# Layer 3 experts: the second product of each pass by seven block products in place of eight

## The chip, the cores and the metric

The kernel runs on one core of a Trainium2 chip. A core has five engines that work side by side: TensorE (matmuls; the trace shows its weight loads as a lane of their own), VectorE, ScalarE, GpSimd and SyncE (here it only issues transfers). The data lie in on-chip memory (SBUF), the results of matmuls in accumulation banks (PSUM), and everything large in the chip's main memory, from where DMA brings it. The metric is the device time of one execution in microseconds. The time of the kernel before is the median of three runs, 3683.46 us (3682.76 to 3685.95).

## The reference, cut to what matters

The whole computation has four layers on 4096 tokens of 256 channels. The change is in the last one, the mixture of experts of layer 3:

```python
TOP_K = 2                                  # x: 4096 tokens x 256, E = 8 experts, hidden size 1024
top_w, top_i = top_k(xf @ Wg + bg, TOP_K); top_w = softmax(top_w)
w_dense = sum(one_hot(top_i, E) * top_w[..., None], axis=1)
for e in range(E):
    h = gelu(xf @ W1[e] + b1[e], approximate=False)
    out = out + w_dense[:, e:e+1] * (h @ W2[e] + b2[e])
```

Each token goes to two of eight experts. An expert is two matrix products: 256 to 1024 with a gelu behind it (the first product), then 1024 to 256 (the second product), a bias, and the token's weight. The kernel computes in float32.

## The kernel before, in words

The kernel sorts the tokens by expert ahead of the experts' work (`route`, `tile_table`): 8192 pairs of token and expert stand in a table `xs` in main memory, each expert's rows together. `experts` then goes over passes of 256 rows each (`MT = 256`, so `NI = 2` blocks of 128 tokens). There is room for 39 passes; the first 36 (`MOST`) always run, the others only where the counts of tokens ask for them, and here they don't.

One pass, in `expert_tiles`, has these parts:

- `load(i)` issues three transfers on SyncE, in the order of that queue: 256 rows `x`, the expert's `w1` (1028 KB in the page) and `w2` (1152 KB), two passes ahead. `w1` and `w2` have three buffers each, so a load waits until the pass that read the buffer last is done with it.
- `turn(x)` (L1928, L1930): four 128x128 transposes on TensorE, one copy on VectorE to `f_xT`.
- `first(xT, w1)` (L146 with `f_h_ps`, L1940): eight chunks of 128 hidden units. A chunk is two matmul calls of 256 columns into half a bank of `f_h_ps`, then one activation on ScalarE (gelu and bias) to `f_h`. Two chunks share one bank, there are three banks, and a matmul into a bank waits for the activation that reads the other half of it.
- `where(i, x)` (L1948 to L1956): nine tiny VectorE operations which work out each row's weight `f_wgt` and its destination `f_at`.
- `second` (L146 with `f_y_ps`, L1964, L1966, L1967): for each of two blocks of 128 tokens eight accumulating matmul calls, with 128 hidden units by 128 tokens of `f_h` as the loaded weights and 256 columns of `f_w2` streamed past them; one VectorE addition of the bias over 128x512; two ScalarE scalings by the rows' weights; and two indirect transfers from GpSimd's queue, which scatter the rows into `ys`.

The loop at the end of `expert_tiles` is skewed by one pass: in the round of pass i TensorE does the first product of pass i, the transposes of pass i+1 and the second product of pass i-1. The build puts the instructions of each engine into an order by its own plan, so that order differs in places from the source: it is the order in which each engine, strictly one after the other, executes. `where` for example stands one round early, and L1948 waits for rows `x` whose load is issued in the same round.

After the last pass the rows of `ys` are read back, added to the tokens, transposed and written out.

A float32 matmul call shows in the trace as two records (two weight loads, two matmuls): the 16 calls of a second product are "x32". A record's duration runs to the modelled end of the pipeline, so the pace is read from the starts of successive records, not from the durations.

Of the kernel before, what the change touches and what calls it, by code (L numbers as in the profile page):

```python
# [10 lines left out]
F32 = mybir.dt.float32  # L11
# [3 lines left out]
ALU = mybir.AluOpType  # L15
# [4 lines left out]
P = 128  # L20
C = 256
# [28 lines left out]
NI = MT // P  # L50
# [30 lines left out]
def bc(ap, axis, n):  # L81

    ap = ap.unsqueeze(axis)
    shape = list(ap.shape)
    shape[axis] = n
    return ap.to_broadcast(shape)


class Net:
# [1813 lines left out]
    def expert_tiles(self, S, tiles, wp, ps):  # L1903
        nc, A = self.nc, self.A
        L, tab = S["L"], S["tab"]
        hidden = 256 if L == 2 else 1024
        KH = hidden // P
        ahead = 3 if L == 2 else 2
        why = "worked out from counts of tokens"

        def load(i):
            e = nc.values_load(tab[0:1, 0, i : i + 1], engines=[mybir.EngineType.SP], min_val=0, max_val=(NE - 1) * P,
                               skip_runtime_bounds_check_because=why)
            row = nc.values_load(tab[0:1, 1, i : i + 1], engines=[mybir.EngineType.SP], min_val=0, max_val=NE * N - MT,
                                 skip_runtime_bounds_check_because=why)
            x = wp.tile([P, NI, CX], F32, tag="x", name="f_x", bufs=ahead + 3)
            nc.sync.dma_start(out=x, in_=self.xs[bass.ds(row, MT), :].rearrange("(i p) c -> p i c", p=P))  # L1917
            w1 = wp.tile([P, 2 * hidden + KH], F32, tag="w1", name="f_w1")
            nc.sync.dma_start(out=w1, in_=A[f"f{L}_w1"][bass.ds(e, P), :])
            w2 = wp.tile([P, KH * C + C], F32, tag="w2", name="f_w2")  # L1920
            nc.sync.dma_start(out=w2, in_=A[f"f{L}_w2"][bass.ds(e, P), :])
            return x, w1, w2

        def turn(x):
            p = ps.tile([P, 2, MT], F32, tag="x", name="f_x_ps", bufs=2)
            for k in range(2):
                for i in range(NI):
                    nc.tensor.transpose(p[:, k, i * P : (i + 1) * P], x[:, i, k * P : (k + 1) * P], self.ident)  # L1928
            xT = wp.tile([P, 2, MT], F32, tag="xT", name="f_xT")
            nc.vector.tensor_copy(xT, p)  # L1930
            return xT

        def first(xT, w1):
            h = wp.tile([P, KH, MT], F32, tag="h", name="f_h")
            for m in range(KH):
                if m % 2 == 0:
                    p = ps.tile([P, 2, MT], F32, tag="h", name="f_h_ps", bufs=3)
                q = p[:, m % 2, :]
                self.mm(q, [(w1[:, kt * hidden + m * P : kt * hidden + (m + 1) * P], xT[:, kt, :]) for kt in range(2)])
                nc.scalar.activation(h[:, m, :], q, AF.Gelu, bias=w1[:, 2 * hidden + m : 2 * hidden + m + 1])  # L1940
            return h

        def where(i, x):

            tl = lambda tag, dt=F32: wp.tile([P, NI], dt, tag=tag, name="f_" + tag, bufs=4)
            first, second, to, wgt, at = tl("first"), tl("second"), tl("to"), tl("wgt"), tl("at", I32)
            op = nc.vector
            op.tensor_scalar(first, x[:, :, C + 3], S["ex"][:, i : i + 1], None, ALU.is_equal)  # L1948
            op.tensor_scalar(second, first, -1.0, 1.0, ALU.mult, ALU.add)
            op.tensor_tensor(wgt, second, x[:, :, C + 2], ALU.mult)  # L1950
            op.tensor_scalar(second, second, float(N), None, ALU.mult)
            op.tensor_tensor(to, x[:, :, C], second, ALU.add)
            op.tensor_tensor(to, to, S["in"][:, i, :], ALU.mult)
            op.tensor_tensor(at, to, S["off"][:, i, :], ALU.add)
            op.tensor_tensor(first, first, x[:, :, C + 1], ALU.mult)
            op.tensor_tensor(wgt, wgt, first, ALU.add)  # L1956
            return at, wgt

        def second(i, h, w2, at, wgt):
            p = ps.tile([P, NI, C], F32, tag="y", name="f_y_ps", bufs=2)  # L1960
            y = wp.tile([P, NI, C], F32, tag="y", name="f_y")
            for k in range(NI):
                self.mm(p[:, k, :], [(h[:, m, k * P : (k + 1) * P], w2[:, m * C : (m + 1) * C]) for m in range(KH)])
            nc.vector.tensor_tensor(y, p, bc(w2[:, KH * C :], 1, NI), ALU.add)  # L1964
            for k in range(NI):
                nc.scalar.mul(y[:, k, :], y[:, k, :], wgt[:, k : k + 1])  # L1966
                nc.gpsimd.indirect_dma_start(  # L1967
                    out=self.ys_parts[(i % 4) * NI + k], in_=y[:, k, :], in_offset=None,
                    out_offset=bass.IndirectOffsetOnAxis(ap=at[:, k : k + 1], axis=0),
                )  # L1970

        tiles = list(tiles)
        ld = {i: load(i) for i in tiles[:ahead]}
        xT = turn(ld[tiles[0]][0])
        to = where(tiles[0], ld[tiles[0]][0])
        done = None
        for i in tiles:
            if i + ahead <= tiles[-1]:
                ld[i + ahead] = load(i + ahead)
            x, w1, w2 = ld.pop(i)  # L1980
            h = first(xT, w1)
            now = (i, h, w2) + to
            if i < tiles[-1]:
                xT = turn(ld[i + 1][0])
                to = where(i + 1, ld[i + 1][0])
            if done is not None:
                second(*done)
            done = now
        second(*done)
# [518 lines left out]
```

## Time and profile before

| what | value |
|---|---|
| time, median of three | 3683.46 us |
| span of the profiled run | 3747.9 us |
| experts of layer 3, first matmul to last matmul | 3172.7 to 3696 us of that span |
| one round in the steady part (start of `f_h_ps` to the next start) | 14.49 us |
| of it: first product, transposes, second product | 7.14, 0.44, 6.91 us |
| matmul records of 128x256 in each product of the stage | 1152 |
| VectorE busy in a round | 17% |
| ScalarE busy in a round | 30% |
| GpSimd busy in a round | 14% |
| DMA engines busy in a round | 52% |

The profiled run is longer than the timed ones; the shares and durations of a stage are what is read from it. A row of the timeline gives the start in us, the length in us, the engine, line and operation, output and inputs, the tile's shape, the number of merged instructions, and in brackets how long the engine had been idle and what ended that. A row of the groups gives the busy time, the mean duration in ns, and the idle time ahead of the group with its releasers. A row of the windows gives, for a stretch of the span, the busy time of each engine with the number of instructions, the granted clock of TensorE, the share of the DMA engines and GB/s.

### The profile page before, as it was taken

The numbers are of one execution on the slowest core, as the hardware profiler recorded it, in microseconds if no ns is written. First come the engines' busy times: TensorE is split into PE (matmuls) and PEld (weight loads), VectorE is DVE, ScalarE is ACT, GpSimd is POOL, SyncE is SP. The second block draws the span as 40 slices with busy tenths as digits, with TensorE's granted clock in tenths as the row PEclk, the third lists the DMA queues.
The fourth block names the chain that finished last, engine by engine and source line by source line (L and its number), as shares of the span: only waits on it lengthen the run. The fifth ranks groups of instructions, "written<-read, shape, count | busy, mean of one in ns | idle before, by whom it ended". The sixth has DMA issues, their size and how long they took to land. (4 is left out here: it accounts for less than half of the span.)

```text
span 3747.9 us, 60403 instructions
## 1 busy us (share of the span) xinstructions
PE 3391.5 (90%) x22708; PEld 2386.9 (64%) x22708; DVE 2183.0 (58%) x5386; ACT 1389.2 (37%) x2845; POOL 1412.2 (38%) x1403
## 2 busy tenths in 40 slices
PE   6989999999997788887786967999999996999997
PEld 4433333333343688855665755888888885888886
DVE  6756656666565477778544557777777775111111
ACT  5544343343432566433332333222222222323231
POOL 1038888888885355534223433000000001111110
PEclk9999999999998899999886989999999997999998
DMA  1014414401013322200013865233223322545454
GB/s 57 3 28 115 132 38 119 124 24 41 21 41 101 108 68 74 77 19 1 13 38 127 262 213 208 86 101 96 93 88 101 97 90 110 196 179 204 180 202 166
DMA packets 160979, 378.33 MB, mean 101 GB/s; under 512 B 17377, under 2 KB 75490, under 8 KB 151458
## 3 DMA queue, kind: packets, MB, share of 16 engines
q1 hardware_dynamic: 136450, 318.96, 26.5%
q0 software_dynamic: 13056, 35.93, 2.5%
q10 hardware_dynamic: 11168, 19.42, 1.5%
q8 instruction: 185, 3.03, 0.3%
q14 instruction: 120, 0.98, 0.1%
HBM read 273.96 MB, written 100.29 MB: 100 GB/s over the span
## 5 line engine op out<-in xcount | busy, mean ns | idle before, releaser
L584 POOL TENSOR_TENSOR l_sm<-l_sc,mask 128x512 f32<-128x512 f32 (+3 forms) x624 | 770.0, 1268 | 120.0 <-ACT l_sc L574 117.6
L578 DVE TENSOR_TENSOR l_sm<-l_s,mask 128x256 f32<-128x256 f32 (+3 forms) x1248 | 492.5, 448 | 301.5 <-PE l_s L568 291.8
L574 ACT COPY l_sc<-l_s 128x384 f32<-128x384 f32 (+3 forms) x896 | 367.7, 461 | 558.5 <-PE l_s L568 543.6
L568 PE MATMUL l_s<-l_q,l_k 32*128 32x384 f32 (+2 forms) x3584 | 424.9, 514 | 7.4 <-ACT l_sc L574 4.1
L1826 POOL DMA_INDIRECT xs<-f_n,f_to x64 | 63.3, 990 | 789.0 <-DVE a_qt L2138 577.5
L146 PE MATMUL f_h_ps<-f_xT,f_w 128*128 128x256 f32 x1440 | 345.4, 388 | 15.6 <-DVE f_xT L1930 7.7
L1967 POOL DMA_INDIRECT ys<-f_y,f_at x144 | 138.7, 963 | 576.6 <-ACT f_y L1966 531.4
L146 PE MATMUL f_y_ps<-f_w,f_h 128*128 128x256 f32 x1440 | 328.5, 379 | 0.0
L568 PEld LDWEIGHTS l_s<-l_q,l_k 32*128 32x128 f32 x3584 | 165.6, 183 | 241.4 <-issue 124.1
L146 PEld LDWEIGHTS f_h_ps<-f_xT,f_w 128*128 128x128 f32 x1440 | 266.0, 192 | 83.7 <-ACT f_h L1940 21.0
L146 PEld LDWEIGHTS f_y_ps<-f_w,f_h 128*128 128x128 f32 x1440 | 268.6, 190 | 33.8
L2186 ACT ACTIVATE a_e<-a_e 128x512 f32<-128x512 f32 x256 | 156.8, 629 | 242.2 <-DVE a_e L2159 234.9
L953 DVE TENSOR_TENSOR l_pr<-l_vk,l_w_ps 128x1280 f32<-128x1280 f32 x128 | 186.5, 1481 | 55.8 <-PE l_acc_ps L957 37.7
L1940 ACT ACTIVATE f_h<-f_h_ps,f_w 128x256 f32<-128x256 f32 x360 | 163.7, 468 | 133.8 <-PE f_h_ps L146 132.1
L957 PE MATMUL l_acc_ps<-ident,l_pr 128*128 128x128 f32 x1600 | 198.0, 278 | 9.3 <-POOL l_pr L948 9.2
L957 PEld LDWEIGHTS l_acc_ps<-ident,l_pr 128*128 128x128 f32 x1600 | 184.5, 144 | 15.7 <-POOL l_pr L948 11.0
L1966 ACT ACTIVATE f_y<-f_y,f_wgt 128x256 f32<-128x256 f32 x144 | 65.3, 500 | 330.1 <-DVE f_y L1964 298.8
L611 PE MATMUL l_a_ps<-l_sm,l_v 128*32 128x512 f32 (+3 forms) x1408 | 178.7, 530 | 1.6 <-POOL l_sm L584 1.5
L2170 PE MATMUL a_sa_ps<-a_q,a_kt 128*128 128x256 f32 x512 | 155.4, 385 | 18.6 <-DMA a_kt<-a_kd 9.6
L611 PE MATMUL l_b_ps<-l_sm,l_v 128*32 128x256 f32 (+2 forms) x2176 | 171.5, 376 | 0.5 <-POOL l_sm L584 0.5
L2174 ACT COPY a_u<-a_sa_ps 128x256 f32<-128x256 f32 x128 | 47.6, 372 | 328.2 <-PE a_sa_ps L2170 325.0
L1964 DVE TENSOR_TENSOR f_y<-f_y_ps,f_w 128x512 f32<-128x512 f32 x72 | 49.8, 691 | 193.4 <-PE f_y_ps L146 187.5
(498 smaller groups left out, 6266.7 us busy)
## 6 DMA issues: line engine op xcount, KB each, us to landing
a_kt<-a_kd SPq DMA_DIRECT2D x128, 512.0 KB
f_w<-in_f_w SPq DMA_DIRECT2D x36, 1152.0 KB
f_w<-in_f_w SPq DMA_DIRECT2D x36, 1028.0 KB
xs<-zero SPq DMA_DIRECT2D x8, 4160.0 KB
l_vk<-vt SPq DMA_DIRECT2D x180, 128.0 KB
f_x<-xs SPq DMA_DIRECT2D x72, 260.0 KB
f_w<-in_f_w SPq DMA_DIRECT2D x36, 384.0 KB
l_rcp<-l_recd SPq DMA_DIRECT2D x48, 256.0 KB
```

Source lines behind the costliest of these rows:

```text
L146: self.nc.tensor.matmul(out, lhsT, rhs, start=(i == 0), stop=(i == len(pairs) - 1))
L568: nc.tensor.matmul(s[pair, j], k[hp, key * P : (key + 1) * P], qs[hp], start=True, stop=True)
L574: nc.scalar.copy(sc[:, j], s[1, j])
L578: nc.vector.tensor_tensor(sms[0][:, j, at : at + t * wide].rearrange("p (t n) -> p t n", n=wide), part[:, which, :], mask, ALU.mult)
L584: nc.gpsimd.tensor_tensor(sms[1][:, :, at : at + t * wide].rearrange("p j (t n) -> p j t n", n=wide), part[:, :, which, :], bc(mask, 1, 2) ...
L611: nc.tensor.matmul(out, v[:, key, hp], sms[pair][:, j, base + lo * wide : base + hi * wide], start=not seen[nm], stop=(left[nm] == 0 and h ...
L953: nc.vector.tensor_tensor(pr, vk, bc(held["w"][:, j, dy], 3, D), ALU.mult)
L957: nc.tensor.matmul(acc[:, m, j, :], pf[:, dx, m * P : (m + 1) * P], self.ident, is_transpose=True, start=(j == 0 and dy == 0 and dx == 0 a ...
L1940: nc.scalar.activation(h[:, m, :], q, AF.Gelu, bias=w1[:, 2 * hidden + m : 2 * hidden + m + 1])
L1967: nc.gpsimd.indirect_dma_start(out=self.ys_parts[(i % 4) * NI + k], in_=y[:, k, :], in_offset=None, out_offset=bass.IndirectOffsetOnAxis(a ...
L2170: mm = lambda out, i, right: nc.tensor.matmul(out, A[i], right, start=True, stop=True)
L2186: nc.scalar.activation(e[:, i : i + 3 : 2], e[:, i : i + 3 : 2], AF.Exp, scale=1.0 / 16.0)
```

## The change

The second product is a 256x1024 by 1024x256 product. Cut in two along the tokens, the hidden units and the output channels it is 2x2 blocks times 2x2 blocks: eight block products as usual, or seven by Winograd's form of Strassen's scheme, with sums of blocks ahead of and behind the products. The "blocks" of hidden units are the first four and the last four chunks of 128.

- `sides(w2)`: four sums of weight blocks (`f_wt`, 128x512 each) on GpSimd, once for each pass.
- `seven`: four sums of blocks of hidden units (`f_hs`, 128x512 each) on VectorE; seven block products of four matmul calls each, 128 columns wide, into two banks `f_ya_ps` and `f_yb_ps`; then a copy on ScalarE and five additions on VectorE which join the products to `f_y`.
- The bias is a VectorE addition of its own on `f_y` (128x512, both operands in SBUF). The scalings and the scatter stay.
- Layer 2's experts keep the second product as it was.

```diff
+        def sides(w2):
+            if L == 2:
+                return None
+            wt = wp.tile([P, 4, KH // 2, P], F32, tag="wt", name="f_wt", bufs=2)
+            b = w2[:, : KH * C].rearrange("p (i m j n) -> p i m j n", i=2, j=2, n=P)
+            for out, x, y in ((0, b[:, 0, :, 1], b[:, 0, :, 0]), (1, b[:, 1, :, 1], wt[:, 0]), (2, b[:, 1, :, 1], b[:, 0, :, 1]),
+                              (3, b[:, 1, :, 0], wt[:, 1])):
+                nc.gpsimd.tensor_tensor(wt[:, out], x, y, ALU.subtract)
+            return wt
+
+        def seven(h, w2, wt, y):
+            hs = wp.tile([P, 4, KH // 2, P], F32, tag="hs", name="f_hs", bufs=2)
+            a = h.rearrange("p (i m) (j n) -> p i m j n", i=2, n=P)
+            nc.vector.tensor_tensor(hs[:, 0], a[:, 0, :, 1], a[:, 1, :, 1], ALU.add)
+            nc.vector.tensor_tensor(hs[:, 1], hs[:, 0], a[:, 0, :, 0], ALU.subtract)
+            nc.vector.tensor_tensor(hs[:, 2], a[:, 0, :, 0], a[:, 0, :, 1], ALU.subtract)
+            nc.vector.tensor_tensor(hs[:, 3], a[:, 1, :, 0], hs[:, 1], ALU.subtract)
...
+            pa = ps.tile([P, 4, P], F32, tag="ya", name="f_ya_ps", bufs=2)
+            pb = ps.tile([P, 4, P], F32, tag="yb", name="f_yb_ps")
+            for out, x, z in (
+                (pa[:, 0], a[:, 0, :, 0], b[:, 0, :, 0]), (pb[:, 2], a[:, 1, :, 0], b[:, 1, :, 0]), (pb[:, 1], a[:, 1, :, 1], wt[:, 3]),
+                (pa[:, 2], hs[:, 0], wt[:, 0]), (pa[:, 1], hs[:, 1], wt[:, 1]), (pa[:, 3], hs[:, 2], wt[:, 2]), (pb[:, 0], hs[:, 3], b[:, 1, :, 1]),
+            ):
+                self.mm(out, [(x[:, m], z[:, m]) for m in range(KH // 2)])
...
+            flat = y.rearrange("p k (j n) -> p (k j) n", n=P)
+            nc.scalar.copy(u1, pa[:, 0])
+            nc.vector.tensor_tensor(flat[:, 0], u1, pb[:, 2], ALU.add)
+            nc.vector.tensor_tensor(u2, u1, pa[:, 1], ALU.add)
+            nc.vector.tensor_tensor(u, pa[:, 2:4], bc(u2, 1, 2), ALU.add)
+            nc.vector.tensor_tensor(flat[:, 3], u[:, 1], pa[:, 2], ALU.add)
+            nc.vector.tensor_tensor(flat[:, 1:3], u, pb[:, 0:2], ALU.add)
 
-        def second(i, h, w2, at, wgt):
-            p = ps.tile([P, NI, C], F32, tag="y", name="f_y_ps", bufs=2)
+        def second(i, h, w2, wt, at, wgt):
             y = wp.tile([P, NI, C], F32, tag="y", name="f_y")
-            for k in range(NI):
-                self.mm(p[:, k, :], [(h[:, m, k * P : (k + 1) * P], w2[:, m * C : (m + 1) * C]) for m in range(KH)])
-            nc.vector.tensor_tensor(y, p, bc(w2[:, KH * C :], 1, NI), ALU.add)
+            if L == 3:
+                seven(h, w2, wt, y)
+                nc.vector.tensor_tensor(y, y, bc(w2[:, KH * C :], 1, NI), ALU.add)
+            else:
+                p = ps.tile([P, NI, C], F32, tag="y", name="f_y_ps", bufs=2)
+                for k in range(NI):
+                    self.mm(p[:, k, :], [(h[:, m, k * P : (k + 1) * P], w2[:, m * C : (m + 1) * C]) for m in range(KH)])
+                nc.vector.tensor_tensor(y, p, bc(w2[:, KH * C :], 1, NI), ALU.add)
...
-            now = (i, h, w2) + to
+            now = (i, h, w2, sides(w2)) + to
```

In the order that the build gives each engine, the sums of weights for a pass stand on GpSimd in the round of its own first product, ahead of the scatters of the pass whose second product has just ended. The sums of hidden units stand on VectorE at the end of the same round's first product. So both are placed one round ahead of the products that read them.

## The prediction

> **What bounds the kernel now.** First the page's engine totals and its 40 slices of 93.7 us, to see who is full in the stage that the change touches (slices 34 to 39).
>
> ```profile
> PE 3391.5 (90%) x22708; PEld 2386.9 (64%) x22708; DVE 2183.0 (58%) x5386; ACT 1389.2 (37%) x2845; POOL 1412.2 (38%) x1403
> ...
> PE   6989999999997788887786967999999996999997
> PEld 4433333333343688855665755888888885888886
> DVE  6756656666565477778544557777777775111111
> ```
>
> TensorE is at 9 from slice 34 on, VectorE at 1. A window of the steady part says it without rounding (columns: PE, weight loads, VectorE, ScalarE, GpSimd, clock, DMA share, GB/s):
>
> ```profile
> 3300.00:3400.00 100.00, 100.00 (x471) 85.28 (x470) 16.94 (x77) 30.24 (x69) 13.54 (x14) 1.00 0.53 194
> ```
>
> A hundred per cent busy isn't yet peak pace, so next the timeline of one round:
>
> ```profile
> 3414.22 7.31 PE L146 MATMUL f_h_ps<-f_xT,f_w 128*128 128x256 f32 x32
> 3414.42 0.69 DVE L1964 TENSOR_TENSOR f_y<-f_y_ps,f_w 128x512 f32<-128x512 f32 x1 [4.06 <-PE f_y_ps L146]
> 3415.19 0.91 ACT L1966 ACTIVATE f_y<-f_y,f_wgt 128x256 f32<-128x256 f32 x2 [7.65 <-DVE f_y L1964]
> 3415.97 0.97 POOL L1967 DMA_INDIRECT ys<-f_y,f_at  x1 [12.26 <-ACT f_y L1966]
> 3416.01 0.81 ACT L1940 ACTIVATE f_h<-f_h_ps,f_w 128x256 f32<-128x256 f32 x2
> 3416.51 4.61 PEld L146 LDWEIGHTS f_h_ps<-f_xT,f_w 128*128 128x128 f32 x22 [0.38 <-ACT f_h L1940]
> 3421.36 0.60 PE L1928 MATMUL f_x_ps<-ident,f_x 128*128 128x128 f32 x4
> 3421.80 7.07 PE L146 MATMUL f_y_ps<-f_w,f_h 128*128 128x256 f32 x32
> ...
> 3423.77 0.16 DVE L1954 TENSOR_TENSOR f_at<-f_to,f_off 128x2 int32<-128x2 f32 x1 [0.75 <-DMA ys<-f_y,f_at]
> 3428.71 7.31 PE L146 MATMUL f_h_ps<-f_xT,f_w 128*128 128x256 f32 x32
> ```
>
> From starts: first product 3421.36-3414.22 = 7.14 us, transposes 0.44, second product 3428.71-3421.80 = 6.91, round 14.49. 6.91/32 is 0.216 us a record; the first product has as many records, so 7.14-6.91 = 0.23 us of it is standstill: the 0.38 at the weight loads, for the first activation, which stands on ScalarE behind the two scalings L1966. Nothing else holds the round: TensorE's pace sets it.
>
> What the new products will cost is read elsewhere, where float32 matmuls already stream 128 columns past fresh 128x128 weights:
>
> ```profile
> 1661.31 1.95 PE L146 MATMUL a_u_ps<-wg_bd,a_vT 128*128 128x128 f32 x16
> 1663.09 7.91 PE L146 MATMUL a_qkv_ps<-w_qkv,a_nT 128*128 128x512 f32 x24
> ```
>
> (1663.09-1661.31)/16 = 0.111 us a record, weight loads included.
>
> **What the skill says.** The Trainium skill, "TensorE: Matmul & The Clock Gate", section "Back-to-back issue gap", gives N/2.4 + 2.5 ns between matmuls. The trace agrees if a float32 record takes two cycles a column: 512/2.4+2.5 = 215.8 (216 here), 256/2.4+2.5 = 109.2 (111 here). The same section warns that with weight loads in the stream a bf16 matmul of 128 columns comes every 81 ns, not 56; section "LDWEIGHTS (loading the stationary operand)" gives columns/1.2, so 107 ns for 128. At 111 ns a float32 load just fits behind its predecessor: no room, but no loss in the trace. "SBUF — State Buffer", section "Who interferes with whom", says that a VectorE operation with two SBUF inputs contends with a GpSimd operation that reads SBUF, and one with a single SBUF input doesn't. The trace agrees; it shows such a pair, where VectorE's 128x256 takes 0.69 in place of 0.42 (L2190's mean is 424 ns):
>
> ```profile
> 2239.32 0.45 POOL L2150 TENSOR_TENSOR a_vs<-a_vs 128x128 f32<-128x128 f32 x1
> 2239.36 0.69 DVE L2105 TENSOR_TENSOR a_ks<-a_ks 128x256 f32<-128x256 f32 x1
> ```
>
> **The change part by part.** I set t = 0 at the first matmul of a round's first product; the round's second product ends at about 13.6.
>
> *TensorE.* Out: 32 records of 0.216 = 6.91 us. In: 7 products x 4 calls x 2 records = 56 of 0.1117 (mean of 0.111 and the 112 ns that most gaps in that row measure) = 6.25. Saved 0.66 us a pass, 36 passes: 23.8 us. It is an eighth of the columns less the fixed cost of 24 more records. All of it is on the path. Bounds: 0.109 a record (the transposes' pace, 0.44/4) would save 0.80; the warning above, taken as 81/56 x 0.109 = 0.158, would cost 1.9. I take 0.1117, since it is measured for this type and shape.
>
> *Sums of hidden units.* Four VectorE operations of 128x512, 0.69 each (L1964's row) = 2.8 us a round, and nobody waits: in the built order they stand a round ahead of their products, two just before the copy `f_xT` (L1930), two behind it. L1930 moves from about 8.5 us into the round to about 9, and TensorE wants `f_xT` at 13.6. Cost nothing, hidden by the second product.
>
> *Sums of weights.* Four GpSimd operations of 128x512. Nearest row: L1431, 1046 ns (L584, beside VectorE, 1160). So 4.2 to 4.6 us, with the contention up to 5.3. They begin when the buffer of two passes ago is free, at t = -0.7, and end at 3.6 to 4.6. Their reader comes a round later: no cost by themselves. But the two scatters stand behind them on GpSimd and move from t = 1.75 and 3.0 to about 4.4 and 5.7. Who waits for those? L1954, for its buffer, about 6.2 us behind the second scatter's start (3417.25 to 3423.77, less its own issue: here at t = 9.4), now at about 11.9. Behind L1954 on VectorE are the additions that join the products, due at 13.3. It holds by 1.4 us.
>
> *Joining the products.* Before: 0.69 us (L1964), scalings from t = 0.97. After: the copy on ScalarE waits for all four regions of `f_ya_ps`, finished 8 records before the end: t = -0.7. Then copy 0.27 (a 128x128 copy, L574's smallest form, 269 ns), 0.29 (128x128 on VectorE, L578's form, 286), 0.42 (128x256, L2159), 0.29, 0.29, 0.42, with some overlap of neighbours (about 0.08 each, seen in back-to-back rows): t = 1.2. Those have one SBUF input. The bias addition has two, beside GpSimd's sums: 0.69 alone, plus a wait of 0 to one GpSimd operation (1.05); I take 0.5. It ends at t = 2.4 (1.9 to 3.0), the scalings 0.1+0.91 later at 3.4 (2.9 to 4.0).
>
> *What queues behind that on ScalarE.* In the built order two activations now stand ahead of the scalings, and the third (second half of the first bank) behind. The two ahead remove the 0.23 us standstill. The third ends at 3.4+0.45 = 3.8 (3.3 to 4.4); TensorE needs it for the sixth chunk at 5 x 0.864 = 4.3, its weight load 0.2 sooner. So no wait in the middle, 0.3 at the upper end. I take a first product of 7.0 us.
>
> *Loads.* `w2`'s buffer is free after the bias addition: the three loads issue 1.4 us later, from t = 2.3. They are wanted a round later or more; `x` lands about 8.5 in place of 7, and L1948 with the nine tiny operations still ends before 12. The bytes stay, so DMA goes from 52% to about 55%.
>
> *Sum.* Round: 7.0+0.44+6.25 = 13.69 against 14.49. Over 36 second products 23.8; over 35 first products (0.23-0.09) x 35 = 4.9 more; the last pass ends with a longer joining chain, about 1 us lost. 23.8+4.9-1 = 27.7, say 27: **3656 us**.
>
> **Rivals.**
>
> *A: the joining chain stops TensorE.* Contention on more than the bias addition puts the scalings 0.5 us later; then the sixth chunk stands 0.3 to 0.5 us. Two engines stand between the products and the activations where it was one; against it, five of the six operations have a PSUM input. First product 7.3 to 7.4: 23.8-0.2x35-1 = 16, time 3667.
>
> *B: slower than before, by GpSimd.* If a weight sum takes 1.6 us (1.16 with the slowdown of 0.69/0.42), four take 6.4, the second scatter starts at 7.5, L1954 comes at 13.7, the joining moves by 0.5 and all behind it, and standstill reaches 1 us a round: 23.8-0.8x35-1 = -5, time 3689. For it: a queue of three engines in a ring. Against: VectorE has at most one two-SBUF operation while the sums run.
>
> *C: slower, by weight loads.* There are 56 loads in place of 32, and a load fills its record. At 0.14 us a record the second product takes 7.84: +0.93x36-4 = +29, time 3713. Against: the 111 ns measured.
>
> **How the numbers follow.** The forecast has 0.64 (no standstill to 0.2), A 0.22, B 0.09, C 0.05. The fast end is no standstill and 0.109 a record: (0.80+0.2)x36-1 = 35, but with 0.1117 it is 31, 3652; I put the low end at 3650. The upper end takes in A with a margin: 3673. B and C are left out. Faster by over 0.2% (below 3676): 0.86, with all of A bar a tail; within: 0.05; slower: 0.09, from B and C less their mild forms.
>
> **What would show it.** The second product: 56 records with starts 0.111 to 0.113 apart, 6.25 us from its first to the next first product. The first product 6.9 to 7.1 us; more, with weight loads idle for an activation, is A. On VectorE the bias addition at 0.7 to 1.5 us, the joins near 0.29 and 0.42. On GpSimd sums of 1.05 to 1.25; above 1.5, and L1954 idle for the scatter until the second product's end, is B. Records spaced at 0.13 or more are C. It would be wrong if something I hold for hidden, the copy `f_xT`, a weight sum or a load, turned up as the last release of TensorE.

## The result, and the profile after

The changed kernel takes 3663.2 us (median of four runs, 3658.9 to 3665.8), the kernel before 3684.6 in the same comparison: ratio 0.9941, 95% interval 0.9924 to 0.9958. It is 21 us faster; 3656 was forecast, 3650 to 3673 as the range.

First the page of the changed kernel, engine totals and slices, as shown of before:

```profile
PE 3325.9 (91%) x23572; PEld 2364.7 (65%) x23572; DVE 2371.5 (65%) x5710; ACT 1399.9 (38%) x2881; POOL 1615.8 (44%) x1547
...
PE   6989999999999688978696968999999996999997
PEld 4443334333333488865585746888888885988986
DVE  6756656656566467779675566777777776655552
...
POOL 1028889888897255545334442000000001555552
```

VectorE and GpSimd are at 5 in the stage where they stood at 1. GpSimd's slices before:

```profile
POOL 1038888888885355534223433000000001111110
```

TensorE still shows a 9, so the window of the steady part is needed (same columns as before):

```profile
3300.00:3400.00 100.00, 98.53 (x658) 89.34 (x658) 53.30 (x141) 34.54 (x80) 54.27 (x44) 1.00 0.55 201
```

TensorE now has 1.5 us of gaps in 100, which it had not before. From the starts of the products, 33 steady rounds can be laid side by side:

| us | before | after |
|---|---|---|
| second product, every round | 6.91 | 6.25 |
| first product | 7.15 (first three 7.10) | 6.93 in 21 rounds, 7.67 to 7.69 in 11, 7.2 in one |
| round | 14.49 | 13.62 in 21, 14.37 in 11, 13.89 in one |
| the 33 rounds together | 478.1 | 457.9 |
| first matmul of the stage to its last second-product matmul | 523.2 | 501.6 |

The stage explains the result (-21.6 us: -20.3 in the rounds (20.2 between the rounded sums), -1.4 at the end, +0.1 at the start). But the rounds are of two kinds. Here is a short one, from the end of its predecessor to its second product (start, length, engine, operation, idle time before and releaser). The line numbers have moved: L1967 is now the sums of weights, L1974 to L1977 are the sums of hidden units, L1991 to L1996 the copy and the additions that join the products (the joins), L2002 the bias, L2009 the scalings, L2010 the scatters.

```profile
3167.96 0.16 DVE L1954 TENSOR_TENSOR f_at<-f_to,f_off 128x2 int32<-128x2 f32 x1 [1.01 <-DMA ys<-f_y,f_at]
...
3168.41 2.49 POOL L1967 TENSOR_TENSOR f_wt<-f_w 128x512 f32<-128x512 f32 x2 [5.42 <-PE f_ya_ps L146]
3168.41 0.27 ACT L1991 COPY f_u<-f_ya_ps 128x128 f32<-128x128 f32 x1 [5.38 <-PE f_ya_ps L146]
...
3169.05 7.09 PE L146 MATMUL f_h_ps<-f_xT,f_w 128*128 128x256 f32 x32
...
3170.22 1.24 DVE L2002 TENSOR_TENSOR f_y<-f_y,f_w 128x512 f32<-128x512 f32 x1
...
3171.49 0.91 ACT L2009 ACTIVATE f_y<-f_y,f_wgt 128x256 f32<-128x256 f32 x2
...
3174.09 1.25 POOL L2010 DMA_INDIRECT ys<-f_y,f_at  x1 [0.15 <-ACT f_h L1940]
...
3175.64 0.96 POOL L2010 DMA_INDIRECT ys<-f_y,f_at  x1 [0.30 <-issue]
3175.98 0.60 PE L1928 MATMUL f_x_ps<-ident,f_x 128*128 128x128 f32 x4
3176.41 1.06 PE L146 MATMUL f_ya_ps<-f_w,f_h 128*128 128x128 f32 x8
```

And the next one, a long one (the short round's second product ends where its L146 row starts, 3182.67 - 3176.41 = 6.26 us):

```profile
3182.03 2.49 POOL L1967 TENSOR_TENSOR f_wt<-f_w 128x512 f32<-128x512 f32 x2 [5.43 <-PE f_ya_ps L146]
...
3182.31 1.00 DVE L1954 TENSOR_TENSOR f_at<-f_to,f_off 128x2 int32<-128x2 f32 x1 [2.21 <-DMA ys<-f_y,f_at]
...
3182.67 4.50 PE L146 MATMUL f_h_ps<-f_xT,f_w 128*128 128x256 f32 x20
...
3184.72 1.57 DVE L2002 TENSOR_TENSOR f_y<-f_y,f_w 128x512 f32<-128x512 f32 x1
3186.33 0.91 ACT L2009 ACTIVATE f_y<-f_y,f_wgt 128x256 f32<-128x256 f32 x2 [1.26 <-DVE f_y L2002]
...
3187.65 2.46 PEld L146 LDWEIGHTS f_h_ps<-f_xT,f_w 128*128 128x128 f32 x12 [0.88 <-ACT f_h L1940]
```

With t = 0 at the first matmul, as in the prediction: GpSimd's sums start at -0.64 in both. In the short round L1954, which waits for a scatter to land, runs at -1.09 and takes 0.16 us. In the long one the landing is at -0.36, after the sums have begun, and L1954 takes 1.00: it ends at +0.64, where the first sum ends. The joins stand behind it, so L2002 starts at 2.05 in place of 1.17 and takes 1.57 in place of 1.24. The scalings come at 3.66 in place of 2.44, and with them the third activation; the weight loads stand 0.88 us for it. The round loses 0.75. Of the 11 long rounds each begins with an L1954 that started between -0.58 and +0.29; in every short round it had run before -0.64.

The page's groups give the sums (busy us, mean ns, idle before); the second form comes from the groups of 3200 to 3590 us alone, with L2002 and L1954 (their means are over short and long rounds together):

```profile
L1967 POOL TENSOR_TENSOR f_wt<-f_w 128x512 f32<-128x512 f32 x72 | 89.8, 1267 | 212.1 <-PE f_ya_ps L146 200.3
```

```profile
L1967 POOL TENSOR_TENSOR f_wt<-f_w,f_wt 128x512 f32<-128x512 f32 x58 | 85.4, 1473 | 2.3
...
L2002 DVE TENSOR_TENSOR f_y<-f_y,f_w 128x512 f32<-128x512 f32 x28 | 38.1, 1360 | 1.0
...
L1954 DVE TENSOR_TENSOR f_at<-f_to,f_off 128x2 int32<-128x2 f32 x27 | 11.3, 420 | 32.0 <-DMA ys<-f_y,f_at 31.9
```

So a sum takes 1.27 or 1.47 us, not 1.05 to 1.16. The theory for the runs, S: the four sums put the scatters some 3.4 us later on GpSimd (5.0 and 6.6 in place of 1.75 and 3.0), and in a third of the rounds the landing is too late for L1954. Its main rival, K: contention (an operation of one engine held up while the other works) between GpSimd and VectorE makes the joining chain late by itself, and the scatters don't matter.

### The profile page after: what moved, and what is told of

The parts are those of the page before. It is cut to its first block, busy times and chain, and to the rows that moved or that the text cites. A ratio compares the mean times of both kernels' runs of the same rounds, so it can differ in the third digit from the quotient of the medians.

```text
span 3657.2 us, 62647 instructions
## 1 busy us (share of the span) xinstructions
PE 3325.9 (91%) x23572; PEld 2364.7 (65%) x23572; DVE 2371.5 (65%) x5710; ACT 1399.9 (38%) x2881; POOL 1615.8 (44%) x1547
## 5 line engine op out<-in xcount | busy, mean ns | idle before, releaser
L146 PE MATMUL f_h_ps<-f_xT,f_w 128*128 128x256 f32 x1440 | 341.3, 387 | 19.8 <-ACT f_h L1940 10.9
L146 PEld LDWEIGHTS f_h_ps<-f_xT,f_w 128*128 128x128 f32 x1440 | 261.4, 191 | 84.5 <-ACT f_h L1940 33.3
L2010 POOL DMA_INDIRECT ys<-f_y,f_at x144 | 145.3, 1009 | 138.0 <-ACT f_y L2009 107.9
L957 PEld LDWEIGHTS l_acc_ps<-ident,l_pr 128*128 128x128 f32 x1600 | 183.6, 143 | 13.4 <-POOL l_pr L948 8.4
L1967 POOL TENSOR_TENSOR f_wt<-f_w 128x512 f32<-128x512 f32 x72 | 89.8, 1267 | 212.1 <-PE f_ya_ps L146 200.3
L2213 PE MATMUL a_sa_ps<-a_qt,a_kt 128*128 128x256 f32 x512 | 152.7, 380 | 0.0
L2232 DVE TENSOR_TENSOR a_et<-a_e 128x512 f32<-128x512 f32 x128 | 88.6, 692 | 73.6 <-ACT a_e L2229 73.5
L2213 PE MATMUL a_sb_ps<-a_qt,a_kt 128*128 128x256 f32 x512 | 132.0, 380 | 0.0
```

Of the source, the lines that this page charges most:

```text
L146: self.nc.tensor.matmul(out, lhsT, rhs, start=(i == 0), stop=(i == len(pairs) - 1))
L957: nc.tensor.matmul(acc[:, m, j, :], pf[:, dx, m * P : (m + 1) * P], self.ident, is_transpose=True, start=(j == 0 and dy == 0 and dx == 0 a ...
L2213: mm = lambda out, i, right: nc.tensor.matmul(out, A[i], right, start=True, stop=True)
```

## The experiments

Each variant has its ratio to the kernel before, timed beside it on the same chip. That kernel took 3682 to 3743 us on the chips used, the difference lying outside this stage; so ratios and rounds are compared, not times. The rounds are those of one profiled execution of each variant. Where the intervals of two ratios overlap, as those of the changed kernel and e1 do, it is the rounds that tell the two apart.

**e1: eight buffers for the small tiles.** L1954 then waits for a scatter of a much earlier pass.

```diff
-            tl = lambda tag, dt=F32: wp.tile([P, NI], dt, tag=tag, name="f_" + tag, bufs=4)
+            tl = lambda tag, dt=F32: wp.tile([P, NI], dt, tag=tag, name="f_" + tag, bufs=4 if L == 2 else 8)
```

> Of the changed kernel, with eight buffers in place of four for the small tiles of `where`, f_at among them, so that L1954 waits for no scatter. In the changed kernel 12 of 34 rounds have a first product of 7.2 to 7.7 us in place of 6.93. Theory S (late scatter: the GpSimd sums hold back the scatters, L1954 waits for those, the joins stand behind L1954): all rounds 13.6 us, 8.5 us less than the changed kernel, 3654 to 3655 us. Rival K (contention: the bias addition, 1.24 us beside the GpSimd sums in place of 0.69, is what delays the scalings and the third activation): L2002 keeps 1.24 us, a third of the rounds stays at 14.4, 3663 us.

Measured: 3655.8 us, ratio 0.9925 (0.9912 to 0.9938). All rounds are 13.60 to 13.62 but one of 13.90. The first matmul of the stage to its last second-product matmul takes 492.4 us, where the changed kernel takes 501.6. The groups of 3200 to 3590 us show L1954 at its own length, and no wait for a scatter; L2002 is as slow as in a short round:

```profile
L2002 DVE TENSOR_TENSOR f_y<-f_y,f_w 128x512 f32<-128x512 f32 x28 | 34.5, 1231 | 1.0
...
L1954 DVE TENSOR_TENSOR f_at<-f_to,f_off 128x2 int32<-128x2 f32 x27 | 4.3, 161 | 0.9
```

S holds, and K as it was put falls: with L1954 in time, the contention on L2002 is there and costs nothing. No version that computes everything has shorter rounds.

**e3: sums of weights only in the first pass.** All later passes read the first pass's sums; GpSimd is left with the scatters alone.

```diff
-            now = (i, h, w2, sides(w2)) + to
+            if i == tiles[0]:
+                wt = sides(w2)
+            now = (i, h, w2, wt) + to
```

> Of the changed kernel, with the sums of weights computed once, for the first pass, and used for all passes: the output is that of wrong weights, the work on GpSimd is four sums in place of 144. S and K both expect no stall: rounds of 13.6 us, 3654 us. A third theory, that the long rounds come from the load of x or from the banks of f_h_ps and not from GpSimd at all, expects a third of the rounds to stay at 14.4 us, 3663 us.

Measured: 3651.2 us, ratio 0.9915 (0.9902 to 0.9928). The same 33 rounds as in e1: 13.60 to 13.62, one of 13.90. The groups of the same stretch:

```profile
L2002 DVE TENSOR_TENSOR f_y<-f_y,f_w 128x512 f32<-128x512 f32 x28 | 19.4, 692 | 1.0
...
L1954 DVE TENSOR_TENSOR f_at<-f_to,f_off 128x2 int32<-128x2 f32 x27 | 4.3, 160 | 7.0 <-DMA ys<-f_y,f_at 6.2
```

So once L1954 is in time the sums cost the rounds nothing. The single round of 13.9 has another cause: it is the same round in the changed kernel, e1 and e3, and in it the first activation on ScalarE starts at t = 1.39 in place of 1.12. Why stays open.

**e5: three buffers for the sums of weights.** The idea was to let the sums start sooner and the scatters with them.

```diff
-            wt = wp.tile([P, 4, KH // 2, P], F32, tag="wt", name="f_wt", bufs=2)
+            wt = wp.tile([P, 4, KH // 2, P], F32, tag="wt", name="f_wt", bufs=3)
```

> Of the changed kernel, with three buffers in place of two for f_wt, so that the sums no longer wait for the products of two passes ago and start when w2 has landed, behind the scatters of the round before. S: the sums run at about 7 to 12 us of the round before, the scatters start with the scalings at about 3 us, L1954 no longer waits to the end of the round: all rounds 13.6 us, 3654 us. K: the bias addition falls to 0.69 us as well, so the same 3654 us; the run tells whether both can be had at no cost on TensorE, or whether the sums beside the sums of hidden units delay f_xT (then rounds above 13.7 us).

Measured: 3680.8 us, ratio 0.9999 (0.9991 to 1.0007): a miss, the whole gain is gone. 32 of 33 rounds take 14.1 to 14.8. The timeline of one round:

```profile
3299.30 3.01 POOL L1967 TENSOR_TENSOR f_wt<-f_w 128x512 f32<-128x512 f32 x2 [2.87 <-DMA f_w<-in_f_w]
...
3301.11 1.23 DVE L1949 TENSOR_SCALAR f_second<-f_first 128x2 f32<-128x2 f32 x1
...
3302.27 3.13 POOL L1967 TENSOR_TENSOR f_wt<-f_w,f_wt 128x512 f32<-128x512 f32 x2
3302.85 1.22 DVE L1950 TENSOR_TENSOR f_wgt<-f_second,f_x 128x2 f32<-128x2 f32 x1
...
3303.95 4.50 PE L146 MATMUL f_h_ps<-f_xT,f_w 128*128 128x256 f32 x20
...
3304.18 1.24 DVE L1956 TENSOR_TENSOR f_wgt<-f_wgt,f_first 128x2 f32<-128x2 f32 x1
...
3305.80 0.28 DVE L1993 TENSOR_TENSOR f_u<-f_u,f_ya_ps 128x128 f32<-128x128 f32 x1
```

The sums no longer wait for TensorE but start when `w2` lands, in the middle of the second product. There VectorE has `where`'s tiny operations, each some 0.16 us when undisturbed. Three of them now take 1.2 us, and each ends with a sum: L1949 ends with the second sum (3301.11+1.23 = 3302.34 against 3299.30+3.01 = 3302.31), L1956 with the last (3305.42 against 3305.40). The joins behind them come at t = 1.85 in place of -0.34. A wait that seemed to hold the sums back had kept them away from VectorE's work.

**e6: the same with eight buffers for the small tiles.** Is e5's loss the scatters' wait, or contention?

> Three buffers for the sums of weights f_wt, which moved these sums into the second product and cost 14.1 to 14.8 us a round when tried with four buffers for f_at; here f_at has eight. Theory C (contention: VectorE's L1953, L1954 and L1977 have two SBUF inputs and are held while GpSimd's sums run, and the joins stand behind them): L1954 no longer waits for a scatter but is held all the same, rounds stay at 14.1 or more, 3675 to 3683 us. Theory S (the wait for a landed scatter alone): rounds of 13.6 us, about 3655 us.

Measured: ratio 0.9999 (0.9990 to 1.0007), all rounds but two at 14.2 to 15.0. C is right in kind; the wait (S) had no measurable part in e5. The operations held are mostly other ones of `where` than the expectation named: in e6's trace L1949 takes over 0.5 us in 30 of 32 rounds, L1950 in 29, L1956 in 25, but L1953 and L1954 in one each.

**The changed kernel again, e7 (the fourth sum computed twice), and e10 (that, with eight buffers).** The edit of e7, and e10 adds that of e1:

```diff
-                              (3, b[:, 1, :, 0], wt[:, 1])):
+                              (3, b[:, 1, :, 0], wt[:, 1]), (3, b[:, 1, :, 0], wt[:, 1])):
```

> The changed kernel once more, so that its variants stand beside it on the same chip. Theory S (the four sums of weights on GpSimd hold the scatters back, and in about a third of the rounds L1954, which waits for a landed scatter, comes too late): again a mixture, some 20 to 24 rounds of 13.6 us and 10 to 14 of about 14.4, time near 3663 us. Rival K (the long rounds come from a chance of that one execution): nearly all rounds 13.6, time near 3655.

> The fourth sum of weights is computed twice, so five GpSimd sums stand ahead of the scatters in each round; what is computed stays the same. Theory S: the scatters start 1.3 to 1.5 us later, so L1954 misses its moment in nearly every round: rounds of 14.4 us or more, 3675 to 3690 us. Rival: GpSimd has room (44% busy), the long rounds have another cause, and the fifth sum hides: the same mixture as in the changed kernel, 3660 to 3666 us.

> Five sums of weights as in the kernel with the doubled sum, and eight buffers in place of four for the destinations f_at, so that L1954 waits for a scatter of an earlier round. What is computed stays the same. Theory S: what the later scatters cost goes away with the wait, rounds of 13.6 us, 3654 to 3659 us. Rival (the fifth sum costs by holding VectorE's operations with two SBUF inputs, not by the scatters): as slow as the five sums with four buffers.

Measured in one group:

| | ratio (95%) | rounds of 13.6 | 14.4 and more | other (13.9) |
|---|---|---|---|---|
| changed kernel again | 0.9952 (0.9939 to 0.9966) | 22 | 10, two of them 15.9 and 16.2 | 1 |
| e7, five sums | 0.9965 (0.9951 to 0.9978) | 15 | 17, one of them 15.7 | 1 |
| e10, five sums, eight buffers | 0.9933 (0.9920 to 0.9947) | 32 | 0 | 1 |

The mixture is a trait of the kernel, not of one execution. A fifth sum makes more rounds long, but 17, not nearly all: S had the direction and missed the size. One reason, read from the trace and not tested: in a long round the next L1954 has 0.75 us more, and at the end of 8 of the changed kernel's 11 long rounds it starts early (-1.9 to -1.0), so a long round often makes the next one short. The rounds of 15.7 to 16.2 begin with an L1954 at +1.1 to +3.2, landings far later than any in the first trace of the changed kernel; what made them so late stays open. With the landing out of the way (e10) even five sums cost nothing. The ratios of the changed kernel and e7 overlap; it is the count of rounds that tells them apart.

**e11: L1954 as an addition and a copy.** Is it the late landing, or that L1954 is then held by a GpSimd sum? The copy has one SBUF input where L1954 has two; its row is L1955.

```diff
-            op.tensor_tensor(at, to, S["off"][:, i, :], ALU.add)
-            op.tensor_tensor(first, first, x[:, :, C + 1], ALU.mult)
+            op.tensor_tensor(to if L == 3 else at, to, S["off"][:, i, :], ALU.add)
+            (op.tensor_copy(at, to) if L == 3 else None), op.tensor_tensor(first, first, x[:, :, C + 1], ALU.mult)
```

> The changed kernel, with L1954 split: the addition goes into f_to, which no scatter reads, and a copy with one SBUF input writes f_at. The copy waits for the landed scatter as L1954 did and has the same four buffers; what is computed stays the same. Theory H (the long rounds come from L1954 being held for the first of GpSimd's sums because it has two SBUF inputs; the landing itself is only some tenths of a us late): the copy takes 0.1 to 0.2 us wherever it falls, all but two or three rounds are 13.6 us, ratio to the kernel before 0.992 to 0.9935. Rival W (the late landing alone makes the joins late enough): the same mixture as in the changed kernel, a third of the rounds at 14.4, ratio 0.994 to 0.9955.

Measured: ratio 0.9954 (0.9941 to 0.9968), 21 short and 11 long rounds, as in the changed kernel (two of the long ones take 18.9 and 17.8, with the copy starting at +3.3 and +3.1). But this doesn't speak for W, since the copy was held too:

```profile
3289.46 2.49 POOL L1967 TENSOR_TENSOR f_wt<-f_w 128x512 f32<-128x512 f32 x2 [5.42 <-PE f_ya_ps L146]
3289.58 1.17 DVE L1955 CAST f_at<-f_to 128x2 int32<-128x2 f32 x1 [1.02 <-DMA ys<-f_y,f_at]
```

It ends at 3290.75, t = +0.65, like L1954; undisturbed it takes 0.17. The expectation's first half was wrong. The Trainium skill, "SBUF — State Buffer", section "Who interferes with whom", could have told: copies and casts from SBUF can run in a mode with two ports, and then they contend with GpSimd for a pair of ports that the two share; the section names operations with a constant as well (e5's L1949). The prediction gave that section's rule for a single SBUF input without this exception. That this cast ran in such a mode wasn't measured by itself.

**e12: that copy on ScalarE.** The same wait, four buffers, on an engine that by that section waits on nobody.

```diff
-            op.tensor_tensor(at, to, S["off"][:, i, :], ALU.add)
-            op.tensor_tensor(first, first, x[:, :, C + 1], ALU.mult)
+            op.tensor_tensor(to if L == 3 else at, to, S["off"][:, i, :], ALU.add)
+            (nc.scalar.copy(at, to) if L == 3 else None), op.tensor_tensor(first, first, x[:, :, C + 1], ALU.mult)
```

> The changed kernel, with the destinations f_at written by a copy on ScalarE (L1955) in place of VectorE, just ahead of the copy L1991 that opens the joins; f_at has four buffers and the copy waits for the landed scatter as before; what is computed stays the same. Theory H2 (the long rounds come from the write of f_at being held by GpSimd's first sum, so that it ends at 0.64 us whenever it comes after the sum's start; the landing itself would have left the joins only some tenths late): the copy takes 0.2 to 0.3 us wherever it falls, rounds of 13.6 us but for two or three whose scatter lands after the first matmul, ratio to the kernel before 0.992 to 0.9935. Rival W (the late landing alone makes the joins late enough): a third of the rounds at 14.4 or more, ratio 0.994 to 0.9955.

Measured: ratio 0.9933 (0.9920 to 0.9947); 28 rounds of 13.6, five of 14.37. Two starts of a round, first one with the landing at t = -0.16, then one at -0.01:

```profile
3236.00 0.19 ACT L1955 CAST f_at<-f_to 128x2 int32<-128x2 f32 x1 [5.85 <-DMA ys<-f_y,f_at]
...
3236.16 7.09 PE L146 MATMUL f_h_ps<-f_xT,f_w 128*128 128x256 f32 x32
...
3237.89 0.69 DVE L2002 TENSOR_TENSOR f_y<-f_y,f_w 128x512 f32<-128x512 f32 x1
...
3249.77 0.19 ACT L1955 CAST f_at<-f_to 128x2 int32<-128x2 f32 x1 [6.01 <-DMA ys<-f_y,f_at]
3249.78 4.50 PE L146 MATMUL f_h_ps<-f_xT,f_w 128*128 128x256 f32 x20
...
3251.59 2.94 POOL L1967 TENSOR_TENSOR f_wt<-f_w,f_wt 128x512 f32<-128x512 f32 x2
3251.67 1.74 DVE L2002 TENSOR_TENSOR f_y<-f_y,f_w 128x512 f32<-128x512 f32 x1
```

The cast takes 0.19 wherever it falls, and the eight landings between -0.64 and -0.16 now cost no time. For landings in that stretch, seven of the changed kernel's eleven, it was the hold and not the landing that made the round long. From -0.06 on the landing is late enough without it: e12's five long rounds begin at -0.06 to +0.37, and three of the eleven are of that kind (+0.03, +0.04, +0.29); the last one, at -0.13, lies between. What is left shows the second half of it: L2002, with two SBUF inputs, runs between GpSimd's second and third sum if it starts before the second ends (t = 1.85): at 1.73 it takes 0.69; at 1.89 it is held through the third sum and takes 1.74. In a short round it starts at 1.17, so there is 0.68 us to spare; L1954's hold uses up 0.88.

**e2: the sums of weights on VectorE.**

```diff
-                nc.gpsimd.tensor_tensor(wt[:, out], x, y, ALU.subtract)
+                nc.vector.tensor_tensor(wt[:, out], x, y, ALU.subtract)
```

> The four sums of weights on VectorE in place of GpSimd; what is computed stays the same. In the built order three of them stand among the joins of the products. Theory Q (what is put ahead of the joins or among them moves the scalings and with them the third activation): three sums of about 0.7 us each make the scalings 2 us later, TensorE stands in the first product, rounds of 14.4 to 15.5 us, 3680 to 3710 us; the scatters start right behind the scalings, and no wait of L1954 for them is left. Rival (only the scatters' place behind GpSimd's sums costs time): rounds of 13.6 us, about 3655 us.

Measured: ratio 0.9945 (0.9931 to 0.9958), 27 rounds of 13.86 to 13.88, the others 13.99 to 14.48; neither theory's number. The scalings start at t = 4.05, 1.6 us later than in a short round, as Q said, but the build put four activations ahead of them in place of two, and the weight loads stand only 0.40:

```profile
3355.38 0.89 ACT L2009 ACTIVATE f_y<-f_y,f_wgt 128x256 f32<-128x256 f32 x2
...
3356.69 1.59 PEld L146 LDWEIGHTS f_h_ps<-f_xT,f_w 128*128 128x128 f32 x8 [0.40 <-ACT f_h L1940]
```

Q's last point was wrong: the second scatter starts at 6.1, only 0.5 us sooner than in the changed kernel, and L1954 still comes late in five of the six other rounds. These show what being late costs when no GpSimd sum runs: L1954 takes 0.16 wherever it falls, at -0.34 the round takes 13.99, at +0.14 it takes 14.48, so it pays for lateness one to one. (The sixth, 14.16, is the round that takes 13.9 elsewhere.)

So on VectorE the sums cost 0.26 us in nearly every round, on GpSimd 0.75 in a third of them: about the same.

**e8 and e9: the 0.23 us of standstill in the kernel before.** e8 gives `f_h_ps` four banks in place of three; e9 four banks with one chunk in each, so that no two chunks share a bank (layer 3 only).

```diff
-                    p = ps.tile([P, 2, MT], F32, tag="h", name="f_h_ps", bufs=3)
+                    p = ps.tile([P, 2, MT], F32, tag="h", name="f_h_ps", bufs=3 if L == 2 else 4)
```

> Of the kernel before, with four banks in place of three for f_h_ps in layer 3. It tells how much of the gain comes from the activations that now stand ahead of the scalings (0.23 us a round) and not from the products. Theory: with a free fourth bank TensorE need not wait for the first activation, rounds of 14.26 us (64 x 0.216 + 0.44), 8 us less than before, 3676 us. Rival: the build orders the first chunks so that the wait stays, 3684 us.

```diff
-                if m % 2 == 0:
+                if m % 2 == 0 and L == 2:
                     p = ps.tile([P, 2, MT], F32, tag="h", name="f_h_ps", bufs=3)
-                q = p[:, m % 2, :]
+                if L == 3:
+                    p = ps.tile([P, 2, MT], F32, tag="h", name="f_h_ps", bufs=4)
+                q = p[:, m % 2 if L == 2 else 0, :]
```

> The kernel before, with a bank of its own for each chunk of hidden units (four banks) in layer 3, so that a matmul no longer waits for the activation of the other half of its bank. Theory (the 0.23 us of standstill in the first product comes from two halves sharing a bank, with the scalings ahead of the activation): first product 6.92, round 14.26, ratio to the kernel before 0.998, some 8 us less. Rival (the standstill comes from elsewhere, or returns as a wait for a whole bank): first product 7.15, ratio 1.000.

Measured: e8 ratio 1.0002 (0.9994 to 1.0010), first product 7.15 as before; e9 0.9977 (0.9969 to 0.9985), first product 6.91 in every steady round. The weight loads still wait in e8, and run through in e9:

```profile
3410.55 4.61 PEld L146 LDWEIGHTS f_h_ps<-f_xT,f_w 128*128 128x128 f32 x22 [0.37 <-ACT f_h L1940]
```

```profile
3402.05 6.88 PEld L146 LDWEIGHTS f_h_ps<-f_xT,f_w 128*128 128x128 f32 x32
```

The standstill is the wait between two halves of one bank: in e9 the scalings still stand ahead of the first activation, and it is gone. That in the changed kernel it is the two activations ahead of the scalings that remove it is read from the traces; no run moved them alone. The kernel before could have had 0.24 x 33 = 8 us of the new one's gain without any new product.

## Why the prediction was right, and where not

*The second product.* Taken and measured: 6.25 us, in every steady round; 33 x 0.66 = 21.8 saved. The warning of 81 ns for bf16 didn't carry over, and rival C falls.

*The first product.* "I take a first product of 7.0 us": 6.93 in the undisturbed rounds, and e9 shows that the old standstill is the wait of one half of a bank for the activation of the other. But 11 rounds at 7.68 and one at 7.2 make the 33 first products together 1.4 us longer than before (21 x 6.93 + 11 x 7.68 + 7.2 = 237.2 against 235.8), where the sum had them 4.9 shorter over 35. This difference of 6.3 us is what lies between the 27.7 of the sum and the 21.4 measured.

*The step that failed* is "It holds by 1.4 us", on L1954. Three terms of it were off. The sums: 1.05 to 1.16 taken, 1.27 and 1.47 measured, so the four take 5.5 us, above the upper bound of 5.3, and the second scatter starts at 6.6 in place of 5.7. The landing: one value, 6.2 us, was taken from one round, in which L1954 starts 6.5 us behind the second scatter's start. Over its rounds the trace of the kernel before has 5.4 to 7.7; with 7.7 no margin would have been left (5.7 + 7.7 = 13.4, due at 13.3). After the change it is 4.6 to 8.2, so L1954 comes at 12.4 in a middling short round and at 13.9 in the worst one. And the price of being late: I charged lateness one to one ("the joining moves by 0.5"), which is what e2 shows without sums on GpSimd; beside them L1954 and L2002 are each held to the end of a sum, so that 0.3 us too late becomes 1.22 us at the scalings. The bound "VectorE has at most one two-SBUF operation while the sums run" overlooked L1954, which I had placed ahead of them. The outcome is rival B's mechanism in a third of the rounds, at 0.75 us each.

*Luck.* That the time still lies in the range is in part luck. The range was widened for A, and B, which is nearer to what happened, was left out of it. Nothing in the prediction says how many rounds would be long: with 33 long ones the rounds would have saved 33 x (14.49 - 14.37) = 4 us in place of 20, and with none (e1) the stage took 9 us less.

*The joining chain.* L2002 was put at 0.69 plus 0.5: 1.23 in e1, with the joins at 0.28 and 0.42 as forecast; ScalarE's third activation is in time. Rival A, contention inside the joining chain, falls as a cause of its own: e1 and e3 have L2002 at 1231 and 692 ns and the same rounds. Its sign, weight loads idle for an activation, did appear in the long rounds; that sign can't tell A from B, and it was e1 that did. The two-input rule of the Trainium skill's section agrees with the trace on L2002.

*Hidden parts.* The sums of hidden units, the copy `f_xT` and the loads were never what TensorE or its weight loads waited for in the steady rounds; right. The loss of 1 us in the last pass was wrong: from the last round's start to the last matmul of the stage it takes 19.3 us against 20.7 (two second products are in it, 1.3 of the difference), and what follows is 51.8 us long against 52.0.

## What to carry to other kernels

Give a tile that an asynchronous write still reads so many buffers that its next writer never waits at the end of a round: one number in a pool (e1) took another 9 us off a stage from which the whole change took 22 (501.6 to 492.4, after 523.2). Where VectorE and GpSimd both work from SBUF, look for a small operation that can arrive late: here one that came 0.3 us after a GpSimd sum had begun was held until that sum ended, and whatever was queued behind it with it. Such holds are counted by instruction ends, not by busy shares. And before taking a wait away, see which collision it prevents (e5).

## What was not expected of the hardware

- A VectorE operation on 128x2 elements, 0.16 us alone, takes up to 1.26 (e7) beside a GpSimd sum of 1.27 us, and a cast and an operation with constants, with one SBUF input, are held in the same way (e11: 1.17, e5's L1949: 1.23), where joins with one SBUF and one PSUM input keep their 0.28 and 0.42 us.
- Float32 matmuls of 128 columns with a fresh 128x128 weight load each start 111 or 112 ns apart over the 56 records of a second product (all but two of 1980 gaps of the stage, 109 and 118 ns).
- In e7, whose second scatter starts 1.4 us later, the landing didn't always move by as much: L1954 still starts at -1.5 to -0.8 in many short rounds, 4.1 to 4.8 us behind the scatter in place of 5.8. What in the transfers around it decides the landing stays open.
